# A graph layer's last 426 edges, put into the last columns of a full group's place, with group 200 as a 99th set

## The chip, the cores and the metric

One core of one Trainium2 chip runs the kernel. The metric is the device time of one execution in microseconds (us), as the median of several runs. Beside it stands one execution recorded by the hardware profiler. The engines are named as in the profile: PE (TensorE) multiplies matrices, with PEld for its weight loads; DVE (VectorE), ACT (ScalarE) and POOL (GpSimd) work on elements; SP (SyncE) issues transfers (DMAs). POOL issues the gathers here. Each engine takes its instructions in the order in which they were written.

## The reference

The kernel computes one layer of a graph network: 6250 nodes and 206250 edges with 64 features. The edges are sorted by `dst`; both directions of 100000 random pairs are in them, and a loop at each node.

```python
def ref(x, edge_index, edge_attr, W1, b1, W2, b2):
    src, dst = edge_index[0], edge_index[1]
    msg = relu(x[src] + edge_attr)
    agg = segment_sum(msg, dst, num_segments=x.shape[0])
    h = x + agg
    h = relu(h @ W1 + b1)
    return h @ W2 + b2

h = maximum(layernorm(x, axis=-1), 0.0)
out = x + ref(h, edge_index, edge_attr_64, W1, b1, W2, b2)
```

## The kernel before

**Groups.** A group is 1024 edges: 128 partitions (`P`) of 8 columns (`G`). There are 201 full groups (`NG` = 201, numbered 0 to 200), and 426 edges are left over; they are group 201 (`g == NG`). In its place, they take four columns (`CT` = 4): three columns of 384 edges, and one of the last 128 edges, of which 86 rows (`TD`) repeat edges that the three columns have and are masked out. The node numbers of all edges stand in `src_sb` and `dst_sb`, 1608 columns (`C`) for the full groups and four more.

**What is done for a group.** `load` fetches the edge features (`ea`, one DMA on SP) and gathers the rows `h[src]` of the group into `xg`, one indirect DMA of POOL for each column of 128 edges (`gather`, L160). `take` copies `ea` into a PSUM tile `full` (ACT, L456), `messages` adds the gathered rows to it (DVE, L464) and applies Relu (ACT, L469), `one_hot` writes a 0/1 matrix of each edge's place in a window of 48 nodes (DVE, L440), `window_sum` sums the messages by node with a chain of matmuls, one for each column (PE, L478), and `sum_into_z` adds the window to the running result `z` (DVE, L435). `hidden`, `result` and `store` then compute the two dense layers for a block of 512 nodes as soon as all its edges are summed (L486 to L510); `blocks_behind` calls them.

**Sets: PE gathers too.** From group 4 to group 199, two neighbouring groups are a set (`k = g // 2`, `K0` = 2 up to `K1` = 100, 98 sets). Of an even group the last four columns (`EVEN`) and of an odd group the last two (`ODD`) are not gathered by POOL but by PE, six columns (`T`) of a set. So POOL gathers 4 + 6 columns of a set, and all 8 columns of the groups outside of sets. PE's gather of a set has these steps, each in its own function:

- `hold` and `mask` (DVE, L333, L340, L343), `source` (PE six matmuls L351, ACT L353, then a DMA out and a DMA back that lays the numbers on all partitions, `sources`): which node stands on which of 128 places of each of ten parts of the nodes.
- `find` (DVE, five instructions L370): the 0/1 matrices `found`; `slots_of` (PE, 50 matmuls, L386) takes the rows of `hp` out by them, two parts at a time into a PSUM tile `rows`, and `slots_out` (ACT, five casts, L394) puts them into `picked`. `hp` holds the nodes' rows as three bf16 terms.
- `spot` (a DMA of a row of places), `back` (DVE, ten instructions, L378): the 0/1 matrices `backs`; `room` (ACT, L403) copies the edge features of two columns into a PSUM tile `pick` of two buffers, and `pick` (PE, L412, ten matmuls for a column) lays the rows on the edges. `messages` sums the terms and the feature into `full` with one reduction for two columns (DVE, L466).

Before the loop, `ranks` works out each edge's place in its part (`place`, `part`, `node`) for all sets at once, by tiles of 588 columns (98 sets of six) and in two halves of 294; an edge that gets no place is masked out of the window sums and found again by `find_left`. `find_left` also counts edges outside of their window. If there are any, a second, slow pass runs at the end (`tc.If`).

**The order.** The order is written out by hand in `half(g)`, called for each group in turn: it enters the gather of group g + 6, sums group g - 2 into `z`, makes the messages of group g, the window sum of group g - 1, the pick of group g + 1, and in between the steps of the sets k + 1, k + 2 and k + 3. Groups 0 to 3 and the sets' first steps come ahead of it. `is_set(k)` decides which of the steps there are. The tiles `ea` and `xg` have nine buffers each, so POOL can run at most nine groups ahead of `messages`.

Of the kernel before, what the change touches and what calls it, by code (L numbers as in the profile page):

```python
# [20 lines left out]
P = 128  # L21
# [7 lines left out]
TD = TJ * P - (TE - P)  # L29
C = NG * G  # L30
CT = TJ + 1
W = 48
WB = 512
R = 4
# [12 lines left out]
PART = BB * BN  # L47
EVEN, ODD = 4, 2
T = EVEN + ODD
K0, K1 = 2, NG // 2  # L50
KS = K1 - K0
ROUND = 1.5 * 2 ** 23
BIAS = 4096
# [7 lines left out]
def kernel(  # L61
# [21 lines left out]
    psum = ctx.enter_context(tc.tile_pool(name="psum", bufs=2, space=bass.MemoryType.PSUM))  # L83


    src_sb = const.tile([P, C + CT], I32, name="src_sb")
    dst_sb = const.tile([P, C + CT], I32, name="dst_sb")
    nc.sync.dma_start(out=src_sb[:, :RAW * G], in_=src_main[:, :RAW * G])
    ln_stack = ExitStack()
    lnp = ln_stack.enter_context(tc.tile_pool(name="ln", bufs=2))  # L90
# [58 lines left out]
    def attr_load(ea, g):  # L149
        if g < NG:  # L150
            nc.sync.dma_start(out=ea.rearrange("p j d -> p (j d)"),
                              in_=edge_attr[g * GE:(g + 1) * GE, :].rearrange("(p j) d -> p (j d)", j=G))
        else:
            nc.sync.dma_start(out=ea[:, :TJ].rearrange("p j d -> p (j d)"),
                              in_=edge_attr[C * P:(C + TJ) * P, :].rearrange("(p j) d -> p (j d)", j=TJ))
            nc.sync.dma_start(out=ea[:, TJ, :], in_=edge_attr[E - P:, :])

    def gather(xg, idx, n, rows):
        for j in range(n):
# [84 lines left out]
    def ranks(pool):  # L244
        src_f = pool.tile([P, KS, T], F32, name="src_f")
        nc.vector.tensor_copy(src_f[:, :, :EVEN], of_sets(src_sb, True))
        nc.vector.tensor_copy(src_f[:, :, EVEN:], of_sets(src_sb, False))
        pt = pool.tile([P, KS, T], F32, name="pt")
        whole(pt, src_f, PART)
        nc.vector.scalar_tensor_tensor(src_f, pt, float(-PART), src_f, op0=ALU.mult, op1=ALU.add)  # L250
        yield
        mine = pool.tile([P, SB, KS, T], BF16, name="mine")
        for m in range(SB):
            nc.vector.tensor_scalar(mine[:, m], pt, float(m), None, op0=ALU.is_equal)
        yield
        block = pool.tile([P, KS, T], F32, name="block")
        whole(block, src_f, BN)
        nc.vector.scalar_tensor_tensor(src_f, block, float(P - BN), src_f, op0=ALU.mult, op1=ALU.add)
        nc.vector.tensor_scalar(node, src_f, 1.0, None, op0=ALU.add)
        nc.vector.tensor_copy(part, pt)  # L260
        yield

        where = pool.tile([P, KS, T], F32, name="where")
        for m in range(SB):
            for k in (0, KS // 2):
                ks = slice(k, k + KS // 2)
                before = psum.tile([P, KS // 2, T], F32, name="pick", bufs=2)
                nc.tensor.matmul(before, upper, mine[:, m, ks], start=True, stop=False)
                for d in range(1, T):
                    nc.tensor.matmul(before[:, :, d:], ones_b, mine[:, m, ks, :T - d], start=False, stop=(d == T - 1))  # L270
                if m == 0:
                    nc.vector.tensor_tensor(where[:, ks], before, mine[:, m, ks], ALU.mult)
                else:
                    here = pool.tile([P, KS // 2, T], F32, name="here", bufs=2)
# [13 lines left out]
        return msg  # L288


    left = const.tile([P, C + CT], I16, name="left")
    flag = const.tile([1, 1], I32, name="flag")

    def find_left():
        nc.vector.tensor_scalar(left, slot, 1.0, None, op0=ALU.is_lt)
        nc.vector.scalar_tensor_tensor(left, slot, float(W), left, op0=ALU.is_gt, op1=ALU.add)
        nc.vector.scalar_tensor_tensor(left, dst_sb, 1.0, left, op0=ALU.add, op1=ALU.mult)
        nc.vector.memset(left[:TD, C + TJ:], 0.0)
# [96 lines left out]

    def room(g):

        m = pool_cols(g) if g < NG else G
        _, _, ea, pks = taken[g]
        for i in range(0, G - m, 2):  # L400
            n = min(2, G - m - i)
# [33 lines left out]
        nc.vector.tensor_tensor(z[:, ds(at, W)], z[:, ds(at, W)], aggs.pop(g), ALU.add)  # L435

    def one_hot(g):
        n = G if g < NG else CT
        oh = work.tile([P, G, W], F32, name="oh")
        nc.vector.tensor_tensor(  # L440
            oh[:, :n], slot[:, cols_of(g)].unsqueeze(2).to_broadcast([P, n, W]),
            wslots[:, :W].unsqueeze(1).to_broadcast([P, n, W]), ALU.is_equal)
        hots[g] = oh

# [5 lines left out]
    def take(g):  # L450

        if g <= NG:
            enter(g)
            n = pool_cols(g)
            full = psum.tile([P, G, D], F32, name="full", bufs=2)
            nc.scalar.copy(full[:, :n], taken[g][2][:, :n])  # L456
            taken[g][0] = full

    def messages(g):
        n, m = (G, pool_cols(g)) if g < NG else (CT, CT)  # L460
        full, xg, _, pks = taken.pop(g)
        if g < RAW:
            norm_edges(xg)
        nc.vector.tensor_tensor(full[:, :m], full[:, :m], xg[:, :m], ALU.add)  # L464
# [4 lines left out]
        nc.scalar.activation(msg[:, :n], full[:, :n], AF.Relu)  # L469
        msgs[g] = msg  # L470

    def window_sum(g):
        n, oh, msg = G if g < NG else CT, hots.pop(g), msgs.pop(g)
# [3 lines left out]
        for j in range(n):  # L477
            nc.tensor.matmul(pa, msg[:, j, :], oh[:, j, :], start=(j == 0), stop=(j == n - 1))  # L478
        aggs[g] = pa


# [97 lines left out]
    with tc.tile_pool(name="rank", bufs=1) as rank:  # L579
        steps = ranks(rank)  # L580
        for c in range(0, NB + 1, XC):
# [14 lines left out]
        slot = const.tile([P, C + CT], I16, name="slot")  # L596
# [4 lines left out]
        nc.vector.scalar_tensor_tensor(  # L601
            slot[:, C:], dst_sb[:, C:], 1.0,
            pb[:, NG:NG + 1].to_broadcast([P, CT]), op0=ALU.add, op1=ALU.subtract)
        nc.vector.memset(slot[:TD, C + TJ:], 0.0)
        for g in range(AHEAD):
            enter(g)
        take(0)
# [64 lines left out]
    with tc.If(any_left > 0):  # L672
# [14 lines left out]
        gather(xg, src_sb[:, C:], CT, h_rows)  # L687
        all_windows(combine(xg, ea, CT), left[:, C:], CT)

        for c in range(NB + 1):  # L690
            store(c, *result(c, *hidden(c)))
# [39 lines left out]
```

## Time and profile before

| | |
|---|---|
| time, median of 3 runs | 1386.8 us (1383.34 to 1388.13) |
| the profiled execution | 1385.12 us, of it the span from first to last instruction 1383.3 us |
| mean granted clock of PE | 0.964 of full speed |
| busy: PE, PEld, DVE, ACT, POOL | 1242.3, 1163.1, 1185.2, 508.4, 1022.5 us |
| gathers by POOL: of `x`, of `h_rows` | 32, 992 |

The profile gives, for each line of the kernel and engine, how often an instruction ran, its mean duration, and how long the engine was idle ahead of it and what ended that. An arrow out<-in names the tile that is written and the tiles that are read. "<-issue" is idle time that ends by nothing the profile shows. A timeline lists instructions in order with their start in us from the beginning of the span. The granted clock is the share of full speed at which PE was allowed to run.

### The profile page before, as it was taken

The page shows a single profiled execution, that of the slowest core. Times are in us where ns is not written, and L with a number is a line of the kernel's source. Part 1 is how long each engine was busy: PE and PEld are TensorE (multiplying, and loading weights), DVE is VectorE, ACT ScalarE, POOL GpSimd, SP SyncE. Part 2 cuts the span into 40 slices and gives each one's busy share as a digit, 9 for nine tenths or more (in the row PEclk, how much of TensorE's full clock was granted, in tenths as well). Part 3 has the DMA queues.
Part 4 walks back from the last instruction along what each step waited for, and adds up shares of the span by engine and source line. Part 5 has one row for each costly group of instructions (what it writes and reads, how often), then busy time and mean ns, then how long its engine had stood idle before and what let it go on. Part 6 is the DMA issues. An engine that isn't in the chain of part 4 may idle for free.

```text
span 1383.3 us, 37550 instructions
## 1 busy us (share of the span) xinstructions
PE 1242.3 (90%) x14894; PEld 1163.1 (84%) x14894; DVE 1185.2 (86%) x2847; ACT 508.4 (37%) x1356; POOL 1022.5 (74%) x1035
## 2 busy tenths in 40 slices
PE   1624899999999999999999999999999999989994
PEld 0413799999999999999999999999998998988983
DVE  6765999899899899999898899898998998888972
ACT  2321333433343333443433433334333443333331
POOL 7672777777777777777777777777777777777774
PEclk9766999999999999999999999999999999999996
DMA  5331434434444444444444444444444443443431
GB/s 169 92 71 55 116 86 119 120 100 114 126 118 112 104 116 122 122 117 106 112 117 122 122 108 110 114 119 117 107 112 119 122 118 96 118 119 92 121 75 25
DMA packets 107766, 150.42 MB, mean 109 GB/s; under 512 B 33857, under 2 KB 52673, under 8 KB 107585
## 3 DMA queue, kind: packets, MB, share of 16 engines
q1 hardware_dynamic: 73569, 112.65, 27.5%
q0 software_dynamic: 32768, 33.62, 12.5%
q8 instruction: 118, 1.93, 0.6%
q10 hardware_dynamic: 1248, 1.70, 0.4%
q14 instruction: 63, 0.52, 0.1%
HBM read 144.27 MB, written 3.60 MB: 107 GB/s over the span
## 4 chain that ended last, share of the span: by engine, by line
PE 61%; DMA 8%; POOL 8%; DVE 6%; issue 5%; ACT 2%; DVEq 0%; POOLq 0%; SPq 0%; ACTq 0%
PE pick L412 27%; PE rows L386 21%; PE agg L478 10%; POOL xg L160 8%; DMA xg<-h_rows,src_sb 5%; PE rows L351 2%; DVE backs L378 2%; DVE full L466 1%; DVE found L370 1%; DMA sources<-source_row 1%; PE rows L499 1%; ACT picked L394 1%; PE rows L486 1%; DMA spots<-spot_rows 1%; ACT full L456 1%
## 5 line engine op out<-in xcount | busy, mean ns | idle before, releaser
L160 POOL DMA_INDIRECT xg<-h_rows,src_sb x992 | 987.2, 995 | 334.4 <-issue 264.3
L412 PE MATMUL pick<-picked,backs 128*128 128x192 bf16 x5880 | 517.1, 246 | 23.5 <-ACT pick L403 20.7
L412 PEld LDWEIGHTS <-backs 128*128 128x128 bf16 x5880 | 488.9, 98 | 28.2 <-issue 21.4
L386 PE MATMUL rows<-hp,found 125*128 125x192 bf16 x4900 | 459.8, 247 | 6.5 <-DVE found L370 5.7
L386 PEld LDWEIGHTS <-found 125*128 125x128 bf16 x4900 | 404.8, 98 | 18.3 <-DVE found L370 7.4
L378 DVE TENSOR_SCALAR backs<-spots,ids 128x768 bf16<-128x768 int16 x980 | 335.5, 415 | 0.0
L394 ACT CAST picked<-rows 128x384 bf16<-128x384 f32 x490 | 234.3, 478 | 274.2 <-PE rows L386 269.4
L370 DVE TENSOR_SCALAR found<-sources,nodes_of 125x1280 bf16<-125x1280 int16 x490 | 251.0, 577 | 38.0 <-DMA sources<-source_row 37.6
L466 DVE TENSOR_REDUCE full<-pick 128x128 f32<-128x512 f32 x294 | 205.7, 700 | 67.5 <-PE pick L412 36.0
L478 PEld LDWEIGHTS agg<-oh,msg 128*64 128x64 f32 x3224 | 205.7, 139 | 37.2 <-issue 19.4
L478 PE MATMUL agg<-oh,msg 128*64 128x48 f32 x3224 | 231.0, 226 | 4.3 <-ACT msg L469 4.3
L353 ACT CAST source<-rows 10x128 int16<-10x128 f32 x98 | 25.0, 255 | 456.4 <-PE rows L351 451.8
L469 ACT ACTIVATE msg<-full 128x512 f32<-128x512 f32 x202 | 119.5, 592 | 49.0 <-DVE full L466 26.8
L464 DVE TENSOR_TENSOR full<-full,xg 128x256 f32<-128x256 f32 (+1 forms) x202 | 99.1, 491 | 33.4 <-DMA xg<-h_rows,src_sb 22.8
L440 DVE TENSOR_TENSOR oh<-slot,wslots 128x384 f32<-128x384 int16 x202 | 109.9, 544 | 0.0
L333 DVE TENSOR_TENSOR holds<-place,wslots 128x768 f16<-128x768 f32 x98 | 92.4, 943 | 6.0 <-DMA spot_rows<-sp 6.0
L456 ACT COPY full<-ea 128x256 f32<-128x256 f32 (+1 forms) x202 | 87.2, 432 | 0.0
L403 ACT COPY pick<-ea 128x128 f32<-128x128 f32 x294 | 72.0, 275 | 0.0
L351 PE MATMUL rows<-holds,mask 128*10 128x128 f16 x588 | 49.6, 221 | 4.6 <-DVE mask L343 4.6
L351 PEld LDWEIGHTS <-mask 128*10 128x10 f16 x588 | 31.5, 88 | 21.7 <-issue 19.9
L435 DVE TENSOR_TENSOR z<-z,agg 64x48 f32 x202 | 38.2, 189 | 6.4 <-PE agg L478 3.3
L160 POOL DMA_INDIRECT xg<-in_x_dram,src_sb x32 | 33.4, 1044 | 10.9 <-issue 9.4
(101 smaller groups left out, 284.4 us busy)
## 6 DMA issues: line engine op xcount, KB each, us to landing
ea<-in_edge_attr_dram SPq DMA_DIRECT2D x201, 256.0 KB
sources<-source_row SPq DMA_DIRECT2D x98, 320.0 KB
spots<-spot_rows SPq DMA_DIRECT2D x98, 192.0 KB
xg<-h_rows,src_sb POOLq DMA_INDIRECT x992
source_row<-source SPq DMA_DIRECT2D x98, 2.5 KB
x_sb<-in_x_dram SPq DMA_DIRECT2D x4, 384.0 KB
h_rows<-ln_h SPq DMA_DIRECT2D x4, 384.0 KB
xb<-in_x_dram SPq DMA_DIRECT2D x12, 128.0 KB
```

Source lines behind the costliest of these rows:

```text
L160: nc.gpsimd.indirect_dma_start(out=xg[:, j, :], out_offset=None, in_=rows[:, :], in_offset=bass.IndirectOffsetOnAxis(ap=idx[:, j:j + 1], a ...
L351: nc.tensor.matmul(ps, mk[:, t, :], oh[:, t, :], start=(t == 0), stop=(t == T - 1))
L370: nc.vector.tensor_scalar(found[k][:BN, b].rearrange("p m s -> p (m s)"), row[:BN], nodes_of[:BN, b:b + 1], None, op0=ALU.is_equal)
L378: nc.vector.tensor_scalar(backs[k][:, m].rearrange("p t s -> p (t s)"), row, ids[:, m:m + 1], None, op0=ALU.is_equal)
L386: nc.tensor.matmul(ps[:, i], found[k][:BN, b, m + i, :], hp[:BN, (m + i) * BB + b].rearrange("p t d -> p (t d)"), start=(b == 0), stop=(b ...
L394: nc.scalar.copy(picked[k][:, m:m + n], halves.pop((k, m)))
L412: nc.tensor.matmul(pk[:, u, :3].rearrange("p t d -> p (t d)"), backs[k][:, m, t0 + i + u, :], picked[k][:, m], start=(m == 0), stop=(m == ...
L440: nc.vector.tensor_tensor(oh[:, :n], slot[:, cols_of(g)].unsqueeze(2).to_broadcast([P, n, W]), wslots[:, :W].unsqueeze(1).to_broadcast([P, ...
L456: nc.scalar.copy(full[:, :n], taken[g][2][:, :n])
L466: nc.vector.tensor_reduce(full[:, m + i:m + i + c], pk[:, :c].rearrange("p j t d -> p j d t"), AX.X, ALU.add)
L469: nc.scalar.activation(msg[:, :n], full[:, :n], AF.Relu)
L478: nc.tensor.matmul(pa, msg[:, j, :], oh[:, j, :], start=(j == 0), stop=(j == n - 1))
```

## The change

`CP = C + G`: the 426 edges left over now have the place of a full group, eight columns. Their four columns of edges are the last four of it, and the first four are empty (memsets; slot 1 there, so that nothing is counted as left over). `K1` is 101, so groups 200 and 201 become set 100, the 99th. Of group 200 POOL gathers columns 0 to 3, and of group 201 columns 4 and 5; PE gathers the other six. All functions that took columns 0 to 3 of group 201 take its columns 4 to 7 (`first_col`). The halves of `ranks` are 49 and 50 sets wide, 294 and 300 columns. The first `dst` of group 201 is copied into the first column of its place, from where the window's start is read.

```diff
+CP = C + G
...
-K0, K1 = 2, NG // 2
+K0, K1 = 2, NG // 2 + 1
...
-    src_sb = const.tile([P, C + CT], I32, name="src_sb")
-    dst_sb = const.tile([P, C + CT], I32, name="dst_sb")
+    src_sb = const.tile([P, CP], I32, name="src_sb")
+    dst_sb = const.tile([P, CP], I32, name="dst_sb")
...
+    nc.vector.memset(src_sb[:, C:CP - CT], 0.0)
+    nc.vector.memset(dst_sb[:, C:CP - CT], 0.0)
     for t_sb, tail in ((src_sb, src_tail), (dst_sb, dst_tail)):
         flat = tail.rearrange("p j -> (p j)")
-        nc.scalar.dma_start(out=t_sb[:, C:C + TJ], in_=flat[:TJ * P].rearrange("(p j) -> p j", j=TJ))
-        nc.scalar.dma_start(out=t_sb[:, C + TJ:], in_=flat[TE - P:].rearrange("(p j) -> p j", j=1))
+        nc.scalar.dma_start(out=t_sb[:, CP - CT:CP - 1], in_=flat[:TJ * P].rearrange("(p j) -> p j", j=TJ))
+        nc.scalar.dma_start(out=t_sb[:, CP - 1:], in_=flat[TE - P:].rearrange("(p j) -> p j", j=1))
...
     def pool_cols(g):
-        if g == NG:
-            return CT
         return G - (ODD if g % 2 else EVEN) if K0 <= g // 2 < K1 else G

     def load(g):
         ea = edge.tile([P, G, D], F32, name="ea")
         attr_load(ea, g)
         xg = edge.tile([P, G, D], F32, name="xg")
-        gather(xg, src_sb[:, cols_of(g)], pool_cols(g), x if g < RAW else h_rows)
+        lo = first_col(g)
+        gather(xg[:, lo:], src_sb[:, g * G + lo:(g + 1) * G], pool_cols(g) - lo, x if g < RAW else h_rows)
         return ea, xg

     def cols_of(g):
-        return slice(g * G, g * G + (G if g < NG else CT))
+        return slice(g * G + first_col(g), (g + 1) * G)
+
+    def first_col(g):
+        return 0 if g < NG else G - CT
...
         for m in range(SB):
-            for k in (0, KS // 2):
-                ks = slice(k, k + KS // 2)
-                before = psum.tile([P, KS // 2, T], F32, name="pick", bufs=2)
+            for ks in (slice(0, KS // 2), slice(KS // 2, KS)):
+                n = ks.stop - ks.start
+                before = psum.tile([P, n, T], F32, name="pick", bufs=2)
...
-            n = pool_cols(g)
+            lo, n = first_col(g), pool_cols(g)
             full = psum.tile([P, G, D], F32, name="full", bufs=2)
-            nc.scalar.copy(full[:, :n], taken[g][2][:, :n])
+            nc.scalar.copy(full[:, lo:n], taken[g][2][:, lo:n])
...
-        n, m = (G, pool_cols(g)) if g < NG else (CT, CT)
+        lo, m = first_col(g), pool_cols(g)
         full, xg, _, pks = taken.pop(g)
...
-        nc.vector.tensor_tensor(full[:, :m], full[:, :m], xg[:, :m], ALU.add)
+        nc.vector.tensor_tensor(full[:, lo:m], full[:, lo:m], xg[:, lo:m], ALU.add)
...
-        nc.scalar.activation(msg[:, :n], full[:, :n], AF.Relu)
+        nc.scalar.activation(msg[:, lo:], full[:, lo:], AF.Relu)
...
+        nc.vector.tensor_copy(dst_sb[0:1, C:C + 1], dst_sb[0:1, CP - CT:CP - CT + 1])
         base = const.tile([1, NG + 1], F32, name="base")
...
-        nc.vector.memset(slot[:TD, C + TJ:], 0.0)
+        nc.vector.memset(slot[:TD, CP - 1:], 0.0)
+        nc.vector.memset(slot[:, C:CP - CT], 1.0)
```

`one_hot`, `window_sum`, `attr_load`, `room`, `find_left` and the slow pass change in the same way.

More of the change, by code (lines that the diff above doesn't have):

```diff
@@ L153, in attr_load @@
         else:
-            nc.sync.dma_start(out=ea[:, :TJ].rearrange("p j d -> p (j d)"),
+            nc.sync.dma_start(out=ea[:, G - CT:G - 1].rearrange("p j d -> p (j d)"),
                               in_=edge_attr[C * P:(C + TJ) * P, :].rearrange("(p j) d -> p (j d)", j=TJ))
-            nc.sync.dma_start(out=ea[:, TJ, :], in_=edge_attr[E - P:, :])
+            nc.sync.dma_start(out=ea[:, G - 1, :], in_=edge_attr[E - P:, :])
     def gather(xg, idx, n, rows):
@@ L273, in ranks @@
                 else:
-                    here = pool.tile([P, KS // 2, T], F32, name="here", bufs=2)
+                    here = pool.tile([P, n, T], F32, name="here", bufs=2)
                     nc.vector.scalar_tensor_tensor(here, before, float(m * P), mine[:, m, ks], op0=ALU.add, op1=ALU.mult)
@@ L288, in combine @@
         return msg
-    left = const.tile([P, C + CT], I16, name="left")
+    left = const.tile([P, CP], I16, name="left")
     flag = const.tile([1, 1], I32, name="flag")
@@ L297, in find_left @@
         nc.vector.scalar_tensor_tensor(left, dst_sb, 1.0, left, op0=ALU.add, op1=ALU.mult)
-        nc.vector.memset(left[:TD, C + TJ:], 0.0)
+        nc.vector.memset(left[:TD, CP - 1:], 0.0)
         most = const.tile([P, 1], F32, name="most")
@@ L396, in room @@
     def room(g):
-        m = pool_cols(g) if g < NG else G
+        m = pool_cols(g)
         _, _, ea, pks = taken[g]
@@ L437, in one_hot @@
     def one_hot(g):
-        n = G if g < NG else CT
+        lo = first_col(g)
+        n = G - lo
         oh = work.tile([P, G, W], F32, name="oh")
         nc.vector.tensor_tensor(
-            oh[:, :n], slot[:, cols_of(g)].unsqueeze(2).to_broadcast([P, n, W]),
+            oh[:, lo:], slot[:, cols_of(g)].unsqueeze(2).to_broadcast([P, n, W]),
             wslots[:, :W].unsqueeze(1).to_broadcast([P, n, W]), ALU.is_equal)
@@ L468, in messages @@
         msg = work.tile([P, G, D], F32, name="msg", bufs=3)
-        nc.scalar.activation(msg[:, :n], full[:, :n], AF.Relu)
+        nc.scalar.activation(msg[:, lo:], full[:, lo:], AF.Relu)
         msgs[g] = msg
     def window_sum(g):
-        n, oh, msg = G if g < NG else CT, hots.pop(g), msgs.pop(g)
+        lo, oh, msg = first_col(g), hots.pop(g), msgs.pop(g)
         if g % AB == 0:
@@ L476, in window_sum @@
         pa = banks[-1][:, g % AB]
-        for j in range(n):
-            nc.tensor.matmul(pa, msg[:, j, :], oh[:, j, :], start=(j == 0), stop=(j == n - 1))
+        for j in range(lo, G):
+            nc.tensor.matmul(pa, msg[:, j, :], oh[:, j, :], start=(j == lo), stop=(j == G - 1))
         aggs[g] = pa
@@ L595 @@
         nc.tensor.matmul(pb[:, :NG + 1], ones[0:1, :], base, start=True, stop=True)
-        slot = const.tile([P, C + CT], I16, name="slot")
+        slot = const.tile([P, CP], I16, name="slot")
         nc.vector.scalar_tensor_tensor(
@@ L601 @@
         nc.vector.scalar_tensor_tensor(
-            slot[:, C:], dst_sb[:, C:], 1.0,
+            slot[:, CP - CT:], dst_sb[:, CP - CT:], 1.0,
             pb[:, NG:NG + 1].to_broadcast([P, CT]), op0=ALU.add, op1=ALU.subtract)
-        nc.vector.memset(slot[:TD, C + TJ:], 0.0)
+        nc.vector.memset(slot[:TD, CP - 1:], 0.0)
+        nc.vector.memset(slot[:, C:CP - CT], 1.0)
         for g in range(AHEAD):
@@ L686 @@
         xg = edge.tile([P, G, D], F32, name="xg")
-        gather(xg, src_sb[:, C:], CT, h_rows)
-        all_windows(combine(xg, ea, CT), left[:, C:], CT)
+        gather(xg[:, G - CT:], src_sb[:, CP - CT:], CT, h_rows)
+        all_windows(combine(xg[:, G - CT:], ea[:, G - CT:], CT), left[:, CP - CT:], CT)
         for c in range(NB + 1):
```

## The prediction

> **What bounds the kernel now.** I read the groups of instructions first, for the busiest queues. POOL does nothing but gathers: 992 of `h_rows`, each 995 ns, and ahead of each some 0.3 us in which it waits for nothing that the profile shows.
>
> ```profile
> PE 1242.3 (90%) x14894; PEld 1163.1 (84%) x14894; DVE 1185.2 (86%) x2847; ACT 508.4 (37%) x1356; POOL 1022.5 (74%) x1035
> ...
> L160 POOL DMA_INDIRECT xg<-h_rows,src_sb x992 | 987.2, 995 | 334.4 <-issue 264.3
> ```
>
> So POOL's 74% is really a full queue. The busy time by stretches confirms it: from 175 us to 1369.3 us POOL runs 922 gathers in 1194.3 us, one per 1.295 us, and 0.991 + 0.30 is just that. PE is almost as full (1156.6 of 1194.3 us). The two run in step, and the question is which of them the last stage waits for.
>
> The list of waits says where POOL itself was held: once for 25.9 us and then hardly again. POOL's timeline has that stop at 111 to 137 us, and a last one of 2.42 us ending at 174.86; after it every gap is 0.30 or 0.31. The second line says who waits for POOL: DVE's addition of the gathered rows (L464), 12 times, 22.8 us, 15.3 us of it after 1255.
>
> ```profile
> POOL xg L160 <- DVE full L464: 30.2, 8, 25.9
> ...
> DVE full L464 <- DMA xg<-h_rows,src_sb: 22.8, 12, 4.6
> ```
>
> The timeline of the last 40 us shows the end. Columns: start, duration, engine, line, operation, and in brackets the idle time ahead of it.
>
> ```profile
> 1348.30 0.43 DVE L464 TENSOR_TENSOR full<-full,xg 128x256 f32<-128x256 f32 x1 [1.40 <-DMA xg<-h_rows,src_sb]
> ...
> 1352.20 1.81 PE L412 MATMUL pick<-picked,backs 128*128 128x192 bf16 x20 [0.98 <-ACT pick L403]
> ...
> 1356.08 0.57 DVE L464 TENSOR_TENSOR full<-full,xg 128x384 f32<-128x384 f32 x1 [4.57 <-DMA xg<-h_rows,src_sb]
> ...
> 1358.18 1.11 PE L478 MATMUL agg<-oh,msg 128*64 128x48 f32 x16 [3.11 <-ACT msg L469]
> ...
> 1366.11 0.70 DVE L464 TENSOR_TENSOR full<-full,xg 128x512 f32<-128x512 f32 x1 [8.08 <-issue]
> ...
> 1367.42 1.97 PE L486 MATMUL rows<-z,w_sb 64*64 64x512 f32 x2 [8.13 <-DVE z L435]
> ...
> 1368.29 0.94 POOL L160 DMA_INDIRECT xg<-h_rows,src_sb  x1 [0.30 <-issue]
> ...
> 1370.81 0.43 DVE L464 TENSOR_TENSOR full<-full,xg 128x256 f32<-128x256 f32 x1 [3.44 <-DMA xg<-h_rows,src_sb]
> ```
>
> The four L464 are groups 198 to 201. Each waits for its gather; PE is out of work from 1359.3 to 1367.4. POOL's last twelve gathers (1354.56 to 1369.23) are the eight of group 200 and the four of 201. So the end is POOL's, and there the change takes gathers from it. PE also ends at half clock:
>
> ```profile
> 1359.30:1362.70 3.40, 0.00 (x0) 0.00 (x0) 0.00 (x0) 0.00 (x0) 2.54 (x3) 0.61 0.15 29
> 1362.70:1367.40 4.70, 0.00 (x0) 0.00 (x0) 1.26 (x3) 0.49 (x1) 3.48 (x5) 0.50 0.12 21
> 1367.40:1371.00 3.60, 3.58 (x18) 1.97 (x18) 0.19 (x1) 1.06 (x3) 1.53 (x2) 0.50 0.14 27
> ```
>
> The number after POOL's bracket is the granted clock: it falls in the pause and stays at 0.50. There 16 agg matmuls take 1.94 us, against 1.11 at 1358.
>
> **The change: the set itself.** POOL loses six gathers (group 200 keeps four, group 201 two): 6 x 1.248 = 7.5 us at the unhindered pitch of its last rows (0.945 + 0.30). PE gains 6 matmuls of L351 (0.43 us), 50 of L386 (50 x 0.083 = 4.13) and 60 of L412 (60 x 0.0865 = 5.18, from "x40" in 3.46), 9.7 us, with nothing removed. DVE gains holds 0.94, at and mask 0.43, five found 2.56, ten backs 3.4 and three reductions of 0.70, less 0.4 for smaller L464: 9.0 us. ACT gains one cast of L353 (0.26), five of L394 (2.39) and three copies of L403 (0.82), less 0.3 for smaller L456. SP gains three DMAs (spots, source_row, sources). Behind them in SP's queue stands the load of `xb` for block 11, issued at 1331.2 and not used until 1373.2: a delay of some 10 us is covered. `ea` of group 201 is queued ahead of them.
>
> Where it falls: mask, spot and hold of set 100 lie beside groups 194 and 195, its source beside 196 (PE +0.45 us), its found beside 197, backs and L386 beside 198 and 199. `sources` came 5.6 us after the L351 matmuls for the set before; from about 1339.9 that is 1345.5. found then ends near 1348.1, and DVE meets the rows of group 198 at 1348.85 instead of 1348.30. The 20 matmuls of L386 beside 198 and 30 beside 199 go into PE's own pauses (0.98 and 3.11 us) and into the 8 us behind them, and DVE is done with backs near 1355.5, a little ahead of the rows of group 199. If that cover were gone, backs would push group 199 one for one. So up to group 199 nothing is later than its gather, which POOL brings when it did before: none of the six lies ahead of it.
>
> **The last 27 us.** Let X be the start of L464 for group 199 (before: 1356.08, and 1383.3 - 1356.08 = 27.2 us follow). From X, with each link's duration from the same link a set earlier:
> - L464, L466, then Relu starts at +1.43 (1357.51 before). From Relu to the first pick matmul it took 1.50 us (1345.19 to 1346.69): +2.93. From there to the end of the second reduction 4.26 us (1350.95): +7.19. The rows of group 200 are there: its fourth gather ended at 1359.25 and rows land 1.5 to 1.8 us later, near X + 5.
> - Group 200: Relu at +7.22. To pick of group 201 it was 1.22 us (1350.98 to 1352.20), 0.2 less for a shorter copy: +8.24. Twenty matmuls, 1.73: +9.97. POOL's last gather ends near 1361.8 and its rows are there at about X + 7.3, so here PE and ACT lead, no longer POOL.
> - L486 of block 11, 1.05 at full clock (its two matmuls before): +11.02. Its Relu L491, 0.68 and the gaps, and behind it in ACT's queue the Relu of group 201, 0.38: +12.1. The eight agg matmuls 0.55, L499 1.10 (as 1276.92): +13.8.
> - From the end of L499 (1374.70) to the end it is 8.6 us, a copy, two additions, a store, the `xb` load of 2.33 behind that store, and the last store: +22.4.
>
> PE's longest pause in this is about 1.1 us (ahead of pick for group 200). A pause of 3.11 us left the clock at 1.00 in the row before, so I take full clock, which is 1.4 us of the gain (0.54 on agg, 0.87 on L499).
>
> **What moves X.** Two terms. At the front, 588 columns become 594 and one half 294 becomes 300; the ops on DVE so widened are some 17 wide ones and 18 halves, each by 6 columns, about 6 ns by the widths in the rows (466 ns for 294, 767 for 588): 0.2 us. Four small ops come on top; the two memsets lie in DVE's 5.70 us wait for `x_sb`, the other two cost 0.06 to 0.1 each. DVE's early work sets when POOL is released at 174.86, so 0.4 us count. No row shows whether the memsets wait for the loads of the same tiles: below, nothing; above, 11.3 us (DVE's first reduction of `x_sb` at 8.36 to its cast of `src_sb` at 19.65, which waited for no load). I take nothing: the big load of `src_sb` was issued at 0.83, while the small one into other columns of that tile was in flight until 4.46, so the order is kept by columns.
>
> Second, DVE's added work slows gathers. Beside holds and found the gathers read 1.11 instead of 0.94, beside backs 1.01: 0.17 + 0.17 + 2 x 0.07, at 0.45 us ahead of group 199's rows. The Trainium skill speaks against this change here: "SBUF — State Buffer", section "SBUF: two separate sides", says that the port pair of DVE and GpSimd is held by one instruction for its whole length and the other side blocks fully. The added tensor-scalar work, 6.0 us, meets about five gathers, each losing up to one instruction (0.42 to 0.58): 2.5 us. I take the rows, 0.45, keep 2.5 for the range.
>
> X = 1356.08 + 0.4 + 0.45 = 1356.93, the end 1356.93 + 22.4 = 1379.3 against 1383.3: -4.0 us. The profiled execution took 1385.12 with 1.8 us around its span, 1.7 below the median of 1386.8; I carry the difference over: 1382.8.
>
> **Rivals.**
> POOL keeps the lead: if the links beside group 200 overlap better than I add them, the last gather sets the end. Its rows landed at 1370.8; minus 7.5, plus 0.85 is 1364.2; from there 12.5 us less 1.4 of clock: 1375.3, -8.0 us, 1378.8. For it speaks that POOL led before; against, that the links stand in queue order.
>
> The lock as the page has it: X 2.1 us later than I say, -1.9 us, 1384.9. Against it stand the gather rows.
>
> The other side: the clock falls before group 200's picks. Place: PE's pause between agg of group 198 and pick of group 200. Price: picks +5.2, L486 +0.95, agg of both groups +1.5, L499 +0.87, so 8.5 us: the end is X + 30.9 = 1387.9, +4.6 us, 1391.4. It decides where the pause grows from 1.1 us past 3.1, the longest that kept the clock here (8.1 lost it). For it: the clock once lost was not regained in the 8.6 us from 1367.4 to 1376, though PE was busy for 7.7 of them. The page "TensorE: Matmul & The Clock Gate", Part 1, says that about 3.4 us of busy work bring full clock back; by that rule the price would be some 3 us and the total still a gain of 1. I take the row. Against the rival: three links would all have to slip.
>
> Rows of the new set that don't fit a part's 128 places would start the long second pass; with 768 rows over ten parts, 77 each, I give it nothing.
>
> **How the numbers follow.** About 0.3%, 4.16 us, is what a measurement of this kernel can tell from no change, and my -4.0 stands on that border. The forecast's own case (-6 to -2) has 0.70, split 0.31 faster and 0.39 same; POOL's lead 0.13, faster; the lock 0.07, same; the clock 0.06 and a late front (the memsets) 0.04, both slower. Faster 0.44, same 0.46, slower 0.10. The range reaches down to POOL's lead (1378.5) and up past the lock and a small late front (1388.5); the clock case is left out.
>
> **What would show it.** Right: 986 gathers of `h_rows`, 5940 matmuls of L412, 4950 of L386; POOL done near 1363; L464 of group 199 within 1 us of 1357; granted clock 1.00 until PE's last block; a pick of 20 ending near X + 10. Wrong: DVE's first wait longer than 6 us; L464 of group 199 after 1358.5; a PE pause over 3 us after 1355; DVE waiting for the rows of group 201 rather than for its pick.

## The result, and the profile after

The changed kernel took 1380.62 us (median of 20 runs, 1378.61 to 1384.02) where the kernel before took 1384.82 (20 runs): ratio 0.997, interval 0.9962 to 0.9977, so 4.2 us less. A second measurement gave 0.9958 (0.9944 to 0.9972). The prediction was -4.0 us. The profiled execution has a span of 1380.3 us against 1383.3. Every ratio here compares fast runs with fast runs of the kernel before, measured beside them; nothing is read from one measurement (201 left to POOL, x loaded early) on a chip where the kernel before itself took 2068 us, at a granted clock near 0.84.

The groups of the page show that the change did what it says: six gathers fewer, 60 and 50 matmuls more (the line numbers have moved by 3 to 6: L163 is the gather, L391 `slots_of`, L417 `pick`, L470 and L472 `messages`, L484 `window_sum`, L492 and L505 the matmuls of the two dense layers).

```profile
PE 1251.2 (91%) x15010; PEld 1172.7 (85%) x15010; DVE 1194.2 (87%) x2872; ACT 510.0 (37%) x1365; POOL 1016.6 (74%) x1029
...
L163 POOL DMA_INDIRECT xg<-h_rows,src_sb x986 | 982.1, 996 | 334.1 <-issue 258.6
L417 PE MATMUL pick<-picked,backs 128*128 128x192 bf16 x5940 | 524.0, 246 | 22.2 <-ACT pick L408 19.5
...
L391 PE MATMUL rows<-hp,found 125*128 125x192 bf16 x4950 | 465.2, 248 | 7.0 <-DVE found L375 6.1
```

The end stands in the timelines of PE, POOL and DVE (start, duration, line, operation, and the idle time ahead of it in brackets):

```profile
1355.57 2.64 PE L391 MATMUL rows<-hp,found 125*128 125x192 bf16 x30
1358.14 1.13 PE L484 MATMUL agg<-oh,msg 128*64 128x48 f32 x16
1360.53 3.46 PE L417 MATMUL pick<-picked,backs 128*128 128x192 bf16 x40 [1.25 <-ACT pick L408]
1363.92 1.13 PE L484 MATMUL agg<-oh,msg 128*64 128x48 f32 x16
1365.82 1.81 PE L417 MATMUL pick<-picked,backs 128*128 128x192 bf16 x20 [0.77 <-ACT pick L408]
1367.56 1.07 PE L492 MATMUL rows<-z,w_sb 64*64 64x512 f32 x2
1368.56 1.77 PE L484 MATMUL agg<-oh,msg 128*64 128x48 f32 x24
1370.27 1.10 PE L505 MATMUL rows<-w_sb,h 64*128 64x64 f32 x8
...
1362.37 0.94 POOL L163 DMA_INDIRECT xg<-h_rows,src_sb  x1 [0.30 <-DMA xg<-h_rows,src_sb]
...
1357.60 0.57 DVE L470 TENSOR_TENSOR full<-full,xg 128x384 f32<-128x384 f32 x1 [1.68 <-DMA xg<-h_rows,src_sb]
...
1362.47 0.43 DVE L470 TENSOR_TENSOR full<-full,xg 128x256 f32<-128x256 f32 x1 [2.91 <-DMA xg<-h_rows,src_sb]
...
1365.61 0.30 DVE L470 TENSOR_TENSOR full<-full,xg 128x128 f32<-128x128 f32 x1 [0.27 <-ACT full L462]
1367.72 0.70 DVE L472 TENSOR_REDUCE full<-pick 128x128 f32<-128x512 f32 x1 [1.81 <-PE pick L417]
```

Three things are to be read here. POOL is done at 1363.3, where before it was done at 1369.2. DVE no longer waits for POOL at the last group: the rows of 201 lie ready, and the wait of 1.81 us is for PE's pick. And PE is never idle for more than 1.25 us in these lines, and its granted clock is full through the last full block of 512 nodes (block 11); L505 takes 1.10 us where L499 took 1.97 in the kernel before:

```profile
1371.71 1.09 PE L478 MATMUL agg<-oh,msg 128*64 128x48 f32 x8 [0.45 <-ACT msg L469]
1372.73 1.97 PE L499 MATMUL rows<-w_sb,h 64*128 64x64 f32 x8
```

In the stretches of the changed kernel below, the granted clock is the number ahead of the last two; it falls only in the last stretch shown, behind that block.

```profile
1360.00:1364.00 4.00, 3.47 (x41) 3.31 (x41) 1.13 (x2) 0.67 (x3) 2.71 (x3) 1.00 0.16 29
1364.00:1368.00 4.00, 3.23 (x37) 2.79 (x38) 1.83 (x5) 0.96 (x3) 0.00 (x0) 1.00 0.04 10
1368.00:1372.00 4.00, 3.69 (x36) 2.70 (x34) 1.60 (x6) 1.54 (x4) 0.00 (x0) 1.00 0.00 0
1372.00:1376.00 4.00, 0.40 (x2) 0.26 (x2) 0.68 (x3) 0.28 (x2) 0.00 (x0) 0.70 0.15 46
```

**A measure that moves little.** Two traces of one kernel, which need not come from one chip, differ by up to 2.5 us in when they reach the last groups, so spans of single profiles cannot be compared to the microsecond. X, the start of DVE's addition for group 199, splits a span: what comes after X repeats to 0.3 us in the two kernels that were traced twice. All traces are read by it. POOL's release at the front is the end of its last long wait, near 174 us.

| kernel | POOL released at the front | X | X to the end |
|---|---|---|---|
| before | 174.86 | 1356.08 | 27.2 |
| before, profiled again | 174.47 | 1353.61 | 27.1 |
| changed | 175.20 | 1357.60 | 22.7 |
| changed, profiled again | 173.82 | 1359.55 | 22.5 |
| gathers off, no set | 174.29 | 1354.80 | 21.0 |
| set's work added, all gathers kept | 173.84 | 1357.87 | 26.9 |
| before, PE kept busy by bf16 matmuls | 174.35 | 1358.08 | 27.3 |
| before, PE kept busy by fp32 matmuls | 174.30 | 1358.62 | 26.9 |
| changed, 201 left to POOL | 174.97 | 1356.32 | 22.4 |
| the same, 18 bf16 matmuls added | 174.88 | 1359.97 | 21.6 |
| the same, and x loaded early | 173.60 | 1357.23 | 19.7 |
| 201 left to POOL, x loaded early | 174.10 | 1359.25 | 19.1 |

X follows POOL: in eleven of the twelve traces it lies 1.67 to 1.84 us behind the end of POOL's last gather for group 199. In the run with the set's work added it lies 2.99 us behind, so that run needs a second look below.

### The profile page after: what moved, and what is told of

It reads as the page before. It is cut to its first block, busy times and chain, and to the rows that moved or that the text cites. A ratio compares the mean times of both kernels' runs of the same rounds, so it can differ in the third digit from the quotient of the medians.

```text
span 1380.3 us, 37812 instructions
## 1 busy us (share of the span) xinstructions
PE 1251.2 (91%) x15010; PEld 1172.7 (85%) x15010; DVE 1194.2 (87%) x2872; ACT 510.0 (37%) x1365; POOL 1016.6 (74%) x1029
## 4 chain that ended last, share of the span: by engine, by line
PE 50%; POOL 15%; DMA 12%; DVE 10%; issue 10%; ACT 2%; DVEq 0%; SPq 0%; ACTq 0%; POOLq 0%
PE pick L417 23%; PE rows L391 16%; POOL xg L163 15%; PE agg L484 8%; DMA xg<-h_rows,src_sb 6%; DVE backs L383 3%; DMA ea<-in_edge_attr_dram 2%; DVE full L472 2%; PE rows L356 2%; DMA sources<-source_row 2%; DVE found L375 1%; DMA source_row<-source 1%; PE rows L505 1%; ACT picked L399 1%; DVE full L470 1%
## 5 line engine op out<-in xcount | busy, mean ns | idle before, releaser
L163 POOL DMA_INDIRECT xg<-h_rows,src_sb x986 | 982.1, 996 | 334.1 <-issue 258.6
L417 PE MATMUL pick<-picked,backs 128*128 128x192 bf16 x5940 | 524.0, 246 | 22.2 <-ACT pick L408 19.5
L417 PEld LDWEIGHTS <-backs 128*128 128x128 bf16 x5940 | 495.3, 98 | 26.7 <-issue 20.1
L391 PE MATMUL rows<-hp,found 125*128 125x192 bf16 x4950 | 465.2, 248 | 7.0 <-DVE found L375 6.1
L391 PEld LDWEIGHTS <-found 125*128 125x128 bf16 x4950 | 409.5, 98 | 18.7 <-DVE found L375 7.8
L383 DVE TENSOR_SCALAR backs<-spots,ids 128x768 bf16<-128x768 int16 x990 | 339.5, 415 | 0.0
L472 DVE TENSOR_REDUCE full<-pick 128x128 f32<-128x512 f32 x297 | 207.7, 699 | 72.0 <-PE pick L417 41.4
L484 PEld LDWEIGHTS agg<-oh,msg 128*64 128x64 f32 x3224 | 205.0, 139 | 32.9 <-issue 17.9
L484 PE MATMUL agg<-oh,msg 128*64 128x48 f32 x3224 | 230.2, 225 | 0.6 <-ACT msg L475 0.6
L470 DVE TENSOR_TENSOR full<-full,xg 128x256 f32<-128x256 f32 (+1 forms) x202 | 98.7, 489 | 19.8 <-DMA xg<-h_rows,src_sb 15.4
L163 POOL DMA_INDIRECT xg<-in_x_dram,src_sb x32 | 32.7, 1021 | 11.2 <-issue 9.4
```

The source lines that it names most:

```text
L163: nc.gpsimd.indirect_dma_start(out=xg[:, j, :], out_offset=None, in_=rows[:, :], in_offset=bass.IndirectOffsetOnAxis(ap=idx[:, j:j + 1], a ...
L383: nc.vector.tensor_scalar(backs[k][:, m].rearrange("p t s -> p (t s)"), row, ids[:, m:m + 1], None, op0=ALU.is_equal)
L391: nc.tensor.matmul(ps[:, i], found[k][:BN, b, m + i, :], hp[:BN, (m + i) * BB + b].rearrange("p t d -> p (t d)"), start=(b == 0), stop=(b ...
L417: nc.tensor.matmul(pk[:, u, :3].rearrange("p t d -> p (t d)"), backs[k][:, m, t0 + i + u, :], picked[k][:, m], start=(m == 0), stop=(m == ...
L470: nc.vector.tensor_tensor(full[:, lo:m], full[:, lo:m], xg[:, lo:m], ALU.add)
```

## The experiments

The theory: POOL's last twelve gathers set the end; six of them go, and the chain of the 99th set's steps behind group 199 gives part of that back. The rivals: the set's work costs its busy time; PE's clock is the gain; POOL was late only by accident.

**The gathers by themselves.** The kernel before, with those six gathers left out and nothing in their place (six columns of messages lack the gathered rows).

```diff
-        gather(xg, src_sb[:, cols_of(g)], pool_cols(g), x if g < RAW else h_rows)
+        gather(xg, src_sb[:, cols_of(g)], gathered(g), x if g < RAW else h_rows)
...
+    def gathered(g):
+        return {NG - 1: G - EVEN, NG: CT - ODD}.get(g, pool_cols(g))
...
+        w = gathered(g)
-        nc.vector.tensor_tensor(full[:, :m], full[:, :m], xg[:, :m], ALU.add)
+        nc.vector.tensor_tensor(full[:, :w], full[:, :w], xg[:, :w], ALU.add)
```

> The kernel before, with the six gathers left out that the change takes from POOL (group 200 gathers 4 columns, group 201 two of its four), and no set put in their place: the messages of those six columns lack the gathered rows. It measures what the six gathers are worth by themselves. My theory (POOL's last gather sets the end; the changed kernel gives part of that back through the chain of the 99th set's steps): the last rows land 7.5 us sooner, near 1363.3, and if PE's pause, now some 3.2 us, keeps the clock, another 1.4 us are saved: span 1374.4 to 1375.8, that is -7.5 to -8.9 us, ratio 0.9937 to 0.9946. Rival (the end is set by the chain of group 199 and 200 on DVE, ACT and PE, POOL being late only by accident): no more than the 4 us that the change brought, ratio 0.997.

Measured: ratio 0.995 (0.9933 to 0.9967), and 21.0 us behind X instead of 27.2. DVE's addition for group 201 starts 7.3 us behind X, where before it was 14.7: 7.4 us, against the 7.5 of six gathers. Not all of it arrives at the end, because PE lost its clock sooner, as its timeline in this run shows:

```profile
1356.90 1.92 PE L482 MATMUL agg<-oh,msg 128*64 128x48 f32 x16 [3.32 <-ACT msg L473]
1360.56 1.96 PE L490 MATMUL rows<-z,w_sb 64*64 64x512 f32 x2 [1.73 <-DVE z L438]
1362.45 2.79 PE L482 MATMUL agg<-oh,msg 128*64 128x48 f32 x24
1365.17 1.97 PE L503 MATMUL rows<-w_sb,h 64*128 64x64 f32 x8
```

At half clock these now follow each other without a gap and stand on the path, where before POOL's gathers covered L486. The theory holds in its main point: the gathers are worth 6.2 us behind X and 6.9 in the whole time, more than the 4 of the rival, whose 0.997 lies just outside the interval. Its second point failed: the clock was not kept, and the 7.5 to 8.9 us were not reached behind X. These 6.2 us came although the clock fell 1.3 us behind X (at 1356.1), where in the kernel before it fell 4.0 behind X (at 1360.0), so the clock cannot be the whole gain of the change.

**The work by itself.** The changed kernel, with POOL gathering all twelve columns again; the picked rows are summed into a spare tile.

```diff
+    def gathered(g):
+        return G if g >= NG - 1 else pool_cols(g)
...
-        nc.vector.tensor_tensor(full[:, lo:m], full[:, lo:m], xg[:, lo:m], ALU.add)
+        w = gathered(g)
+        nc.vector.tensor_tensor(full[:, lo:w], full[:, lo:w], xg[:, lo:w], ALU.add)
...
+            to = full[:, m + i:m + i + c] if w == m else work.tile([P, 2, D], F32, name="spare")[:, :c]
```

> The changed kernel with the 99th set's work kept whole, but POOL gathering all eight columns of group 200 and all four of 201 as before; the sums of the picked rows go to a spare tile. It measures what the set's work costs where it relieves nobody. My theory (the work stands in pauses that PE has at the end anyway): X, DVE's addition for group 199, at 1357.6 as in the changed kernel; rows of group 201 near 1372.3; the pick of group 201 ends near 1372.6 and full clock gives 1.4 us back: -0.5 to +2 us, ratio 0.9996 to 1.0015. Rival (the 9.7 us of PE work and 9 us of DVE work lie on the path and the change pays for them out of a larger gain): +5 to +9 us, ratio 1.0035 to 1.0065.

Measured: ratio 0.9998 (0.9984 to 1.0012), 26.9 us behind X. The rival's 1.0035 lies outside: with all of POOL's gathers still there, 9.7 us of PE work, 9 of DVE and 3 of ACT cost at most 1.7 us of the whole time. The 26.9 alone flatters the run, because X was late in it:

```profile
1357.87 0.55 DVE L474 TENSOR_TENSOR full<-full,xg 128x384 f32<-128x384 f32 x1
...
1368.80 3.28 PE L420 MATMUL pick<-picked,backs 128*128 128x192 bf16 x20 [2.79 <-ACT pick L411]
```

L474 for group 199 starts without a pause: DVE was still busy, and the rows were there. In this trace PE was at half clock from 1348.4 to 1351.8, the 40 picks of group 198 took 5.12 us instead of the 3.46 of the changed kernel, and DVE's sums of them and the `backs` behind these in its queue came late and pushed X. PE was at half clock once more from 1368.9 to 1372.3, where the 20 picks of group 201 took 3.28 us instead of 1.81. Counted from POOL's last gather for group 199 the end comes after 29.9 us, and after 29.1 and 28.9 in the two traces of the kernel before: about 1 us later in this trace.

Together with the first run this is the change in its two halves: the gathers take 27.2 to 21.0, and putting the set's work in place of the rows brings 22.5 to 22.7. These 1.5 to 1.7 us are net. The run without the gathers did its last PE work at half clock, the changed kernel at full clock; with the changed kernel's durations for the same links, that run would have ended some 2.5 us sooner, near 18.5 behind X (an estimate from the two traces). By that estimate the set's work costs some 4 us of chain once POOL no longer covers it, and the clock that stays up with it gives some 2.5 of them back.

**The clock by itself.** The kernel before, with 84 matmuls of 192 columns in bf16 in PE's pause of 8 us.

```diff
             window_sum(g - 1)
+        if g == NG - 1:
+            keep = psum.tile([P, 3 * D], F32, name="pick", bufs=2)
+            for _ in range(84):
+                nc.tensor.matmul(keep, ident_b[:BN], hp[:BN, 0].rearrange("p t d -> p (t d)"), start=True, stop=True)
```

> The kernel before, with 84 matmuls of 192 columns added on PE behind the window sum of group 199; nobody reads their result. They fill some 7 us of PE's pause of 8.1 us. It measures the clock by itself. My theory: the granted clock stays 1.00 to PE's last block, L478 of group 201 takes 0.55 us instead of 1.09 and L499 1.10 instead of 1.97: -1.4 us, ratio 0.999. Rival (the change gains because PE stays at full clock, and the gathers count little): -3 to -4 us, ratio 0.9975. Second rival (the clock falls anyway, or the matmuls delay block 11): 0 to +1 us.

Measured: ratio 0.9988 (0.9976 to 1.0), and in the profiled execution nothing, 27.3 us behind X. The clock held through the filler and L486, and yet fell before the block that counts:

```profile
1361.23 7.10 PE L561 MATMUL pick<-hp,ident_b 125*128 125x192 bf16 x84
1370.31 1.07 PE L486 MATMUL rows<-z,w_sb 64*64 64x512 f32 x2 [1.98 <-DVE z L435]
1371.31 1.13 PE L478 MATMUL agg<-oh,msg 128*64 128x48 f32 x16
1373.77 1.09 PE L478 MATMUL agg<-oh,msg 128*64 128x48 f32 x8 [1.33 <-ACT msg L469]
1374.79 1.97 PE L499 MATMUL rows<-w_sb,h 64*128 64x64 f32 x8
```

The eight agg matmuls take 1.09 us and L499 1.97, as at half clock before, though no pause ahead of them was longer than 2 us. The 0.9975 of the rival lies just outside the interval, but this run cannot settle what the clock is worth, not even the 1.4 us that I gave it, since its trace did not bring the clock to the end. That the clock is not the whole gain is shown by the first run, which lost it and gained more.

**What keeps the clock.** From that I took that fp32 matmuls do not count as work for the clock, and ran the kernel before with fp32 matmuls in the pause.

```diff
-            for _ in range(84):
-                nc.tensor.matmul(keep, ident_b[:BN], hp[:BN, 0].rearrange("p t d -> p (t d)"), start=True, stop=True)
+            for _ in range(56):
+                nc.tensor.matmul(keep[:D, :W], ones[:, :D], slots[:, :W], start=True, stop=True)
```

> The kernel before, with 56 matmuls in fp32 of the shape of the window sums (128 rows, 64 columns out, 48 across; nobody reads the result) on PE behind the window sum of group 199, where the warm_pe run had 84 in bf16. The traces so far suggest that PE's clock falls 4 to 6 us after the last bf16 matmul, whatever fp32 matmuls run in between: after 1354.0 before, after 1368.3 with the 84 added, after 1362.6 with group 201 left to POOL. If so (theory now): the clock falls near 1360 though PE is busy, the 56 take more than the 3.7 us of full clock, some 5 to 7 us, and the last block runs at half clock as before: span 1383 to 1385. Rival (any busy PE keeps the clock, only pauses lose it): clock 1.00 until the filler ends near 1363.1.

Measured: that theory fell. The 56 (two records each) ran at full clock for 6.70 us, and so did L486 behind them; the clock again fell only ahead of the last agg.

```profile
1361.67 6.70 PE L561 MATMUL pick<-slots,ones 128*64 128x48 f32 x112
1369.86 1.07 PE L486 MATMUL rows<-z,w_sb 64*64 64x512 f32 x2 [1.50 <-DVE z L435]
1370.86 1.13 PE L478 MATMUL agg<-oh,msg 128*64 128x48 f32 x16
1374.21 1.09 PE L478 MATMUL agg<-oh,msg 128*64 128x48 f32 x8 [2.22 <-ACT msg L469]
```

Nor is it the longest pause alone, as the next run shows. In both of these traces PE had worked for 2.1 of the last 3.4 us when the clock fell; the last section comes back to it.

**Less for PE at the very end.** In the changed kernel DVE waits 1.81 us for the pick of group 201 while POOL has been done for 4.4 us. So group 201 was left to POOL whole.

```diff
     def pool_cols(g):
+        if g == NG:
+            return G
```

> The changed kernel, but group 201 is left to POOL whole (4 gathers, no pick); group 200 keeps its four picked columns. In the changed kernel DVE waits for the pick of group 201 (1.81 us) while POOL is done 4 us earlier. My theory (at the very end ACT and PE lead, and POOL has room for two gathers more): POOL done near 1365.8, rows at 1367.4, no pick and no copy ahead of block 11's matmuls, the end 1.5 us sooner than the changed kernel: span 1378.8, -4.5 to -5.5 us against before, ratio 0.9960 to 0.9967. Rival (each gather at the end costs its 1.25 us, as between before and after): +2.5 us against the changed kernel, ratio 0.9988.

Measured: ratio 0.9957 (0.9938 to 0.9976), 22.4 us behind X. Two gathers more cost nothing, against the rival; but the 1.5 us that I expected on top did not come in this trace, because here, too, the clock was lost, after pauses of 0.34 and 0.93 us only:

```profile
1364.11 1.07 PE L494 MATMUL rows<-z,w_sb 64*64 64x512 f32 x2 [0.34 <-DVE z L442]
1365.11 1.13 PE L486 MATMUL agg<-oh,msg 128*64 128x48 f32 x16
1367.17 1.09 PE L486 MATMUL agg<-oh,msg 128*64 128x48 f32 x8 [0.93 <-ACT msg L477]
1368.19 1.97 PE L507 MATMUL rows<-w_sb,h 64*128 64x64 f32 x8
```

**The same with 18 bf16 matmuls in PE's pauses**, 8 behind the window sum of group 199 and 10 behind that of 200.

```diff
             window_sum(g - 1)
+        if g >= NG - 1:
+            fill(8 if g < NG else 10)
```

> The kernel of the run with group 201 left to POOL, with 8 bf16 matmuls added behind the window sum of group 199 and 10 behind that of group 200, in PE's pauses (result unread). In that run's trace the clock fell ahead of the last window sum: 1.09 us for eight agg matmuls, 1.97 for the eight of the last full block. Theory (bf16 matmuls count and set the clock's time back): both at full clock, 0.55 and 1.10 us, so 1.4 us less: ratio to before some 0.001 under that run's 0.9957. Rival (the pauses decide, or 18 matmuls are too few): no difference, or up to 0.5 us more where a matmul stands in the way.

Measured: ratio 0.996 (0.9945 to 0.9976), no difference from the run without them. In the trace the last block ran at full clock, 21.6 us behind X, 0.8 less than without; the ten stood 0.5 us in the way of the last window sum (1370.18 to 1371.11, while its messages were ready at 1370.57).

**The load that ends last.** DVE waits 3.10 us for the last block's rows of `x` in the changed kernel, since SP issues that load behind the store of block 11:

```profile
1375.33 0.23 DVE L513 TENSOR_TENSOR xb<-xb,b_sb 106x64 f32<-106x64 f32 x1 [3.10 <-DMA xb<-in_x_dram]
```

It was issued ahead of the last window sum, first with the added matmuls, then without.

```diff
+    last_x = rows_of_x(NB)
     window_sum(NG)
...
-    store(NB, *result(NB, *hidden(NB)))
+    store(NB, *result(NB, *hidden(NB, last_x)))
```

> The last run's kernel, and the load of the last block's rows of x issued ahead of the last window sum instead of behind the store of block 11 in SP's queue. In the changed kernel DVE waits 3.10 us for it at the very end. Theory: the wait goes and block 12's store leaves 2.5 us sooner, ratio to before another 0.0018 lower, 0.993 or a little less. Rival (the store itself, or the two stores one behind the other, set the end): less than 1 us.

> The same kernel as in the last call (group 201 left to POOL, the last block's rows of x loaded early, no added matmuls), repeated because the kernel before itself took 2068 us there and nothing can be read from that call. Theory as there: 19.9 us from DVE's addition for group 199 to the end, ratio to before 0.993 to 0.995. Rival (the clock is worth its 1.4 us here): 21 us and 0.996.

Measured: 0.9944 (0.9932 to 0.9957) and 0.9951 (0.9937 to 0.9964), 19.7 and 19.1 us behind X. The wait is gone, some 2 us, and in the timeline of the first of the two kernels DVE's last work follows ACT without a load between:

```profile
1370.98 0.22 DVE L521 TENSOR_TENSOR xb<-xb,b_sb 106x64 f32<-106x64 f32 x1
1371.63 0.23 DVE L522 TENSOR_TENSOR o<-o,xb 106x64 f32<-106x64 f32 x1 [0.43 <-ACT o L515]
```

Without the added matmuls the clock held by itself through the last full block in this trace, where it had been lost in the trace of the run with group 201 left to POOL; the whole times give no sign that the matmuls are needed. This version, group 201 by POOL and the load early, is the best of all: 5 parts in 1000 faster than before, and 3.4 to 3.6 us shorter behind X than the changed kernel. By the whole time it is not told apart from the changed kernel: the intervals overlap that of its second measurement (0.9944 to 0.9972), and barely (0.9964) or not (0.9957) that of its first (0.9962 to 0.9977).

**Both kernels once more.**

> The changed kernel itself, unaltered, beside the others on the same chip. Expected: ratio to before 0.997 as measured first. What is looked for in its trace: POOL's release at the front (175.20 in the first trace, 174.86 before; if the front costs 0.4 us it is again later than before's, if it varies by itself it may lie anywhere in the 173.8 to 175.2 of the other runs), and whether the clock holds to the end once more.

> The kernel before, unaltered, profiled once more. Expected: from DVE's addition for group 199 to the end 27.2 us within 0.5, while the start of that addition (1356.08 in the first trace) moves by 1 us or more; if it stays within 0.3 us, the later starts in the changed kernel's traces (1357.60 and 1359.55) are the change's doing.

Measured: changed 0.9958 and 22.5 us behind X; before 27.1 behind X. Both repeat to some 0.2 us, while X itself moved by 2.0 us in the changed kernel and by 2.5 in the one before, and the release at the front by 1.4 and 0.4. So a later X in a single trace is no proof of a cost. Over all traces X is 1356.2 in the five without the set's work and 1358.3 in the seven with it, 2.0 us later, with 4 to 5 us between the ends of each. POOL's timeline shows how much of that is the set's. From its release at the front to forty gathers ahead of group 199's last one, where nothing of the 99th set runs yet, the traces without it took 1128.6 us on average and those with it 1129.9: 1.3 us, which the added work cannot cause. The last forty gathers took 51.3 to 51.5 us without the set and 51.5 to 52.8 with it, 0.7 us more on average: that is the set's. What is left is the one X that DVE held back, spread over seven traces.

## Why the prediction was right

**POOL sets the end.** Shown: without the six gathers 27.2 becomes 21.0; with them kept and the set's work added, 26.9. One of the four lines read for it does not say so by itself: the addition for group 200 reads 8.08 `<-issue`. That it waited for its rows is told by its start, 1.87 us behind the end of that group's last gather, close to the 1.8 of the addition for group 199.

**The chain behind X.** I predicted 22.4 and the traces have 22.7 and 22.5. The links stand where the sum put them: pick of group 200 at +2.93 (predicted +2.93), Relu of group 200 at +7.21 (+7.22), pick of 201 at +8.22 (+8.24), block 11's matmuls at +9.96 (+9.97), the end of L505 (L499 before) at +13.8 (+13.8). Durations of the same link one set earlier, put in queue order, were enough. Only the last piece was short: 8.9 instead of 8.6, as the last load's wait was 3.10 instead of 2.77.

**The set's work lies in pauses.** Shown by the run that adds it alone, for the whole time: no change, within 1.7 us. But the cover is thin. DVE reached group 199 with 1.68 us to spare in the first trace of the changed kernel, with 0.30 in the second, and in the run that adds the work alone, where PE had lost its clock for 3.4 us, it came some 1.2 us too late, which is the case that I had named, `backs` pushing group 199.

**The terms for X.** X was 1357.60 against my 1356.93, and this agreement means little: in the second trace it was 1359.55, past the 1358.5 that I had called a sign of being wrong. The 0.4 us for the front is not seen: the release averages 174.5 in the traces without the set and 174.3 in those with it. The slower gathers are: the sixteen from group 197 to the start of group 200 took 20.91 us against 20.27, and over all traces the last forty ahead of X took 0.7 us more, where I had 0.45. The gathers beside found and backs read 1.02 to 1.12 us instead of 0.94, so each lost 0.08 to 0.18 us, while one instruction of found or backs takes 0.57 or 0.42 on average. The full block of the shared port, which I had weighed at 2.5 us, did not come; the rows decided rightly. The rest is drift of the whole trace, of which my sum knew nothing: luck that X agreed.

**The memsets.** They ran at 0.93 and 0.95 and waited for no load, as taken.

**The clock.** The number was right and its ground weak. It was full through the last full block in both traces of the changed kernel. But I drew the line at a pause of 3.11 us, and the kernel before lost the clock 0.6 us behind a pause of 3.03 when it was profiled again, and the kernel with group 201 left to POOL after pauses under a microsecond. That a clock once lost does not come back, on which I priced the rival, fell too: with the set's work added, PE lost the clock at 1368.9 us, worked through at half clock and had it back at 1372.3. That is the rule of the Trainium skill's page "TensorE: Matmul & The Clock Gate", Part 1, that I had set aside for the row, so the price of that rival is nearer my 3 us than my 8.5. The rival in which the clock falls before the picks stays possible by what the runs show; it was not seen in any trace of the changed kernel.

**The rivals.** POOL's lead to the end (-8.0 us) fell: DVE waits for PE's pick at the last group. The full lock and the lost clock did not come.

## What to carry to other kernels

Two engines that run in step through the whole kernel need not both be in the way at its end: look at the last waits, and move work from the one that ends last to the one that has a pause there, even if that one is fuller on the page. What the first engine gives up does not all arrive, because the other's chain of short links takes over; add that chain up link by link, in queue order, with the durations of the same links one round earlier. And compare traces by the stretch behind a fixed event, not by their spans, when a few us matter; look each time whether the change itself has moved that event.

## What the runs showed that I had not expected

PE's granted clock can fall without a long pause: with the last picks done at 1362.7 in the run with group 201 left to POOL, two pauses of 0.34 and 0.93 us and 2.1 us of matmuls between, the next ones ran at half speed.

What decides is a fixed beat. In each of the twelve traces the moments at which the granted clock changes lie whole multiples of 3.41 us apart. The Trainium skill's page "TensorE: Matmul & The Clock Gate", Part 1, has a free-running window of some 3.4 us that has to be busy, and the traces agree. A pause therefore costs the clock or not by where it lies. In the first trace of the kernel before the pause of 3.11 us was cut in two by a boundary at 1356.6, the 3.41 us on its left held 1.85 us of PE work, and the clock stayed; in the second the pause of 3.03 lay almost whole in one window with 0.60 us of work, and the clock fell at that window's end, 1356.3. A window in which PE was busy throughout brought it back, as above at 1372.3.

How much work is enough, no run here settles. PE was busy for 0.4 to 2.6 us of the 3.41 ahead of each loss near the end, and 1.85 us were enough in the window above. It is not fp32 alone: the added fp32 matmuls kept the clock in a window with 2.18 us of them, while 2.40 us of the fp32 matmuls of the window sums and the dense layers lost it in the run with group 201 left to POOL.
